# A decoder layer on one core: column means of two weights from a chunk sum, and v transposed at the head of a turn

## The chip, the core and the metric

The kernel runs on one core of one Trainium2 chip. The metric is the device time of one execution in microseconds (us). Engines are named as in the profile: PE is TensorE (PEld its weight loads), DVE is VectorE, ACT is ScalarE, POOL is GpSimd and SP is SyncE, which issues every DMA of this kernel. "L12" is line 12 of the kernel.

## The reference, cut to what matters

A decoder layer in float32 on x of shape (16, 256, 512): a state-space block, a long-convolution block over the other sequence, and a feed-forward block with eight low-rank experts, two of them chosen for each token. Each block is followed by a residual and a layer norm.

```python
x = layernorm(x + ssm(x, ...))
x = layernorm(x + conv_mix(x, k, fside_S2_0, ctx_2048, ctx_2048, 8))
x = layernorm(x + ffn(x, W, b, lora_A, lora_B, gate_w, gate_b))

def conv_mix(v, k, bias, x1, x2, num_heads):      # heads of 8 rows, 32 of them
    kv = vr[:, :, :, None, :] * x2r[:, :, None, :, :]
    y = causal_convolution(kv, k) + kv * skip
    out = einsum("bhijl,bhil->bhjl", y, x1r)

def ffn(x, W, b, lora_A, lora_B, gate_w, gate_b):
    base = x @ W.T + b
    logits = x @ gate_w.T + gate_b                # top 2 of 8, softmax over the two
    xA = einsum("nd,erd->ner", x, lora_A)
    out = base + sum over the chosen e of gate_e * (xA_e @ lora_B_e.T)
```

The layer norm ahead of the feed-forward block is not applied to its input. The kernel takes the column mean out of the weights instead, once: subtracting from each column of W.T (and of the gate and lora_A weights side by side) its mean over the 512 input rows has the same effect as subtracting each token's mean from x. The factor 1/std is multiplied in afterwards.

## The kernel before, in words

The order of the work is written out by hand: each engine executes its instructions in the order in which the code records them (`manual_schedule`), and waits only for data and for buffers. A buffer of a pool is given again when it is free; a new tile waits for the last reader of the tile before.

**First stage.** A loop over eight groups g of 512 tokens. In each group, ten steps i (the list `order`) form one pair of output blocks each, of the kinds x, z, b and c, by a seven-product scheme. Step i records `first_products` of its own pair (8 matmuls of 256 columns), then `finish_products` of the step before (6 matmuls), then the sums on DVE (`first_sums`, L357 to L361; `last_sums`, L371 to L373), and for the kind x the short convolution `mixed` (L571 to L580) into tiles `acc`, a tag of six buffers in pool p2. At step 6 `head_means(0)` (L585 to L596, matmul L589) reads four of these tiles, at step 8 `head_means(1)` the other four.

The weights of the feed-forward block, `w_f` (128 x 4 x 512: the 512 input rows as four chunks of 128 partitions) and `w_gl` (128 x 4 x 136, gates and lora_A), are loaded at the end of g = 0. In g = 1 they are prepared: at step 2 `with_identity` adds the residual's identity to w_f on DVE (L519, L521), and `centred` (L523 to L531) is called at the head of step 5 for w_f and of step 6 for w_gl. It forms the column means in one PSUM tile `mw` by four accumulating matmuls with `share`, a 128 x 128 matrix of 1/512, one for each chunk (L527), and subtracts the tile from each chunk on DVE (L531). POOL has only small operations in this part of g = 1.

**Second stage.** A loop over the 32 heads h (L1198), called turns below. In turn h, two halves q of the head's batch rows are convolved (`convolve`, L1005): matmuls with Toeplitz blocks of the taps, full 128 x 128 ones (L1014) and triangular ones as quadrants of 64 x 64 (L1032), into the PSUM tiles y[0] and y[1]. `contract` on DVE multiplies y by x1 (L1067) and sums (L1077). Meanwhile the feed-forward block of head h - 1 is done in pieces, and the products kv of head h + 1 are formed on DVE (L158) from vT and cT.

At the head of a turn with h > 0 the code records

- `feed_forward(base, o_r, (3,))`: the last of the four matmuls with w_f of head h - 2 (L1193), into PSUM tile `base`, where `rest` is not None (from h = 2);
- `turned_gates(xa)`: a transpose of the weighted low-rank activations on PE (L1183) and the copy `xaT` on ACT (L1185);
- `seeded(y, T, xs, 0)`: a matmul into `yc` (L1002), copied by ACT to both halves of y[1] (L1003), which the full matmuls of `convolve` add to;
- `lora(base, ...)`: a matmul that adds the low-rank part to base (L1189);
- `turned_v` for head h + 1: four transposes of the tile vn on PE (L146) and the copy vT on ACT (L148);
- the loads for later heads on SP: `load_T(h + 1)`, `load_v(h + 2)` into the single buffer of vn, `load_c(h + 2)`.

Then `convolve` for q = 0 begins with L1014 into y[0] and y[1]. The PSUM tiles of the transposes (vn, xa, the feed-forward input o_l at L1104) and of the gate logits `gl` share the two buffers of the tag "tr".

Of the kernel before, what the change touches and what calls it, by code (L numbers as in the profile page):

```python
# [8 lines left out]
F32 = mybir.dt.float32  # L9
AF = mybir.ActivationFunctionType  # L10
ALU = mybir.AluOpType
# [3 lines left out]
P = 128  # L15
B, S, D = 16, 256, 512
KD = D // P
# [14 lines left out]
NE, R = 8, 16  # L32
# [21 lines left out]
ER = NE * R  # L54
# [17 lines left out]
def decoder_kernel(  # L72
# [24 lines left out]
    nc = tc.nc  # L97
# [44 lines left out]
    def turned_v(vn):  # L142

        tr = ps_t.tile([P, NL, P], F32, tag="tr", name="tr")
        for k, blk in enumerate(BLOCKS_IN):
            nc.tensor.transpose(tr[:, k, :], vn[:, blk * P : (blk + 1) * P], ident)  # L146
        vT = q2.tile([P, NQ, NL, BQ * NH], F32, tag="vT", name="vT")
        nc.scalar.copy(  # L148
            vT.rearrange("p q k t -> p k q t"), tr.rearrange("p k (q t) -> p k q t", q=NQ)
        )  # L150
        return vT
# [29 lines left out]
    with ExitStack() as s1:  # L181
# [3 lines left out]
        p2 = s1.enter_context(tc.tile_pool(name="p2", bufs=2))  # L185
# [160 lines left out]
        def first_products(w, p, third, begun=None, between=None):  # L346

            al, be = begun or begin_products(w, p, third)
            product(be[:, 0:S], w, p, S1, "T1", start=True)
            if between is not None:  # L350
                between()
            product(al[:, S:], w, p, S2, "T2", stop=True)
            product(be[:, S:], w, p, S3, "T3", stop=True)
            return al, be
# [157 lines left out]
        def with_identity(w):  # L512

            for k, blk in enumerate(BLOCKS_OUT):
                own = w[:, k, blk * P : (blk + 1) * P]
                if blk in SWAPPED_OUT:
                    for a, b in ((0, HP), (HP, 0)):
                        half = own[:, a : a + HP]
                        nc.vector.tensor_tensor(half, half, ident[:, b : b + HP], ALU.add)  # L519
                else:  # L520
                    nc.vector.tensor_tensor(own, own, ident, ALU.add)  # L521

        def centred(w, cols):  # L523

            ps = ps_t.tile([P, 512], F32, tag="tr", name="mw")
            for kc in range(KD):
                nc.tensor.matmul(  # L527
                    ps[:, 0:cols], share, w[:, kc, :], start=(kc == 0), stop=(kc == KD - 1)
                )
            for kc in range(KD):  # L530
                nc.vector.tensor_tensor(w[:, kc, :], w[:, kc, :], ps[:, 0:cols], ALU.subtract)  # L531

# [6 lines left out]
                nc.sync.dma_start(first[sh][bi], r)  # L539

        heads = {}
        late = []
        for g in range(NG):
            xs = xs_next
            more = g + 1 < NG
# [39 lines left out]
            def head_means(ht):  # L585

                xm = ps_t.tile([P, GT], F32, tag="tr", name="xm")
                for q in range(4):
                    nc.tensor.matmul(  # L589
                        xm[32 * q : 32 * (q + 1), :],  # L590
                        mean.rearrange("p h n -> p (h n)"),
                        accs[4 * ht + q].rearrange("p b s -> p (b s)"),
                        start=True,
                        stop=True,
                    )
                return xm  # L596
# [44 lines left out]
            for i, (kind, p) in enumerate(order):  # L641
                if g == 1 and i == 2:
                    with_identity(w_f)
                if g == 1 and i in (5, 6):
                    centred(*((w_f, D), (w_gl, NE + ER))[i - 5])
                if i == 6:
                    ms = [head_means(0)]
                if g == 0 and i == 0:
                    al, be = first_products(
                        kinds[kind], p, True, None,  # L650
                        lambda: begun.append(begin_products(w_xi, order[1][1], False)),
                    )
                else:
                    al, be = first_products(
                        kinds[kind], p, i % 3 == 0, begun.pop(0) if begun else None
                    )
                if i == 8:
                    ms.append(head_means(1))
                if i == 9:


                    yps = ps_t.tile([P, S], F32, tag="tr", name="yps")
                    for ht in range(HT):
                        for b in range(GB):
                            nc.tensor.matmul(
                                yps[b * HP : (b + 1) * HP],
                                sel[:, ht].rearrange("p q h -> p (q h)"),
                                Bs[ht][:, b * S : (b + 1) * S],
                                start=(ht == 0),
                                stop=(ht == HT - 1),  # L670
                            )
                if before is not None:
                    finish_products()
                to = places(kind, p)
                u = first_sums(al, be, to)
                if i == 8:
                    states(1, stepped(ms[1], spreads[2]), spreads[3])
                if i == 6:
                    ms = [stepped(ms[0], spreads[0])]
                    spreads.append(spread(1, 1))  # L680
                if g == 0:
                    if i == 1:
                        parts = decays()
                    if i == 2:
                        nc.scalar.activation(A, A, AF.Exp)
                        nc.vector.tensor_scalar(A, A, -1.0, None, ALU.mult)
                    if i in (1, 2, 4):
                        next(parts)
                if i == 9:
                    yT = q3.tile([P, S], F32, tag="vn", name="yT", bufs=1)  # L690
                    nc.scalar.copy(yT, yps)
                if before is not None:
                    finish_sums((lambda: next(parts)) if g == 0 and i == 2 else None)
                if g == 0 and i == 3:
                    next(parts)
                if g == 0 and i in later:
                    for n, (w, k) in enumerate(later[i]):
                        ins = weight_sums(nc.gpsimd, w, k)
                        if n == 0:
                            wait_for(ins, mixes[-1])  # L700
                if i == 7:
                    states(0, ms[0], spreads[1])
                if i == 8:
                    outputs(0)
                    outputs(1)
                    if more:
                        rt = to_dram(rms(xs_next))
                    if g == 0:
                        behind = []
                        w_sums = w_o_sums(behind)  # L710
                        next(w_sums)
                before = (kind, p, al, be, u, to)
                if i < 2 and late:
                    normalised(g - 1, late.pop(0))
                if i == 1 and more:
                    xs_next = load_x(g + 1)
# [95 lines left out]
            late = []  # L812
            if more:
# [36 lines left out]
                late = [(1, xs[1]), (3, xs[3])]  # L850
            else:
                finish_sums()
                gated(1, spread_heads(1))
                for n, t in enumerate((0, 2, 1, 3)):


                    ps = ps_s.tile([P, 512], F32, tag="s", name="s") if n in (0, 3) else bank()
                    for c in range(NI):
                        for j in range(2):
# [4 lines left out]
                                start=(c == 0 and j == 0),  # L864
                                stop=(c == NI - 1),
# [14 lines left out]
            if g == 0:  # L880
                skip_bc = wp.tile([P, S], F32, name="skip_bc")
                nc.sync.dma_start(skip_bc, skip.partition_broadcast(P))
                w_gl = wp.tile([P, KD, NE + ER], F32, name="w_gl")
                nc.sync.dma_start(w_gl, WglT.rearrange("(k p) e -> p k e", p=P))
                w_f = wp.tile([P, KD, D], F32, name="w_f")
# [10 lines left out]
                share = wp.tile([P, P], F32, name="share")  # L896
# [5 lines left out]
    with ExitStack() as s2:  # L902
        w2 = s2.enter_context(tc.tile_pool(name="w2", bufs=1, reuse_waits="tile"))
        p2 = s2.enter_context(tc.tile_pool(name="r2", bufs=2, reuse_waits="tile"))
# [254 lines left out]
        vT_next, vns = heads["vT"], heads["vn"]  # L1159
# [38 lines left out]
        for h in range(HX):  # L1198
            nxt, ff = h + 1 < HX, last is not None
# [5 lines left out]
                prs = [multiplied(y_f, cT_f, 1, i) for i in order]  # L1205
            y = new_y()
            if h:
                if rest is not None:
                    base, o_r, xa = rest
                    feed_forward(base, o_r, (3,))  # L1210
                    turned = turned_gates(xa)
                seeded(y, T, xs, 0)
                if rest is not None:
                    lora(base, [turned])
                if nxt:
                    vT_after = turned_v(vns.pop(0))
                    kvs.append(load_T(h + 1))
                    if h + 2 < HX:
                        vns.append(load_v(h + 2))
                        cTs.append(load_c(h + 2))  # L1220
# [13 lines left out]
            if h == 0:  # L1234
                vT_after = vT_ahead[0]
# [212 lines left out]
```

## Time and profile before

| what | value |
|---|---|
| median of 3 runs | 1430.14 us (1429.83 to 1431.35) |
| span of the profiled execution | 1429.6 us; no further time of that execution is listed |
| PE busy, DVE busy | 1415.0 us (99%), 1215.5 us (85%) |
| ACT busy, POOL busy | 461.5 us (32%), 559.8 us (39%) |
| chain that ended last | PE for 96% of the span |
| granted TensorE clock | 0.999 |
| steps 2 to 6 of g = 1 | about 116 to 152 us from the span's start |
| second stage | from about 757 us |
| length of one turn | 20.61 us (L1183 from 1001.55 to 1022.16) |

The span is the time from the first to the last instruction in the profile, and the run times lie a little above it. A group of the profile names the line, the engine, the operation, and the tiles written and read. A float32 matmul leaves two MATMUL records, each with a weight load of its own; the records overlap, so that the time which a matmul holds TensorE is read from start to start. In a timeline, the columns are start, duration from the first to the last of the merged instructions, engine, line, operation, tiles, count, and in brackets the idle time before with what ended it. In a list of waits, the numbers are the total, the count and the longest.

### The profile page before, as it was taken

The numbers are of one execution on the slowest core, as the hardware profiler recorded it, in microseconds if no ns is written. First come the engines' busy times: TensorE is split into PE (matmuls) and PEld (weight loads), VectorE is DVE, ScalarE is ACT, GpSimd is POOL, SyncE is SP. The second block draws the span as 40 slices with busy tenths as digits, with TensorE's granted clock in tenths as the row PEclk, the third lists the DMA queues.
The fourth block names the chain that finished last, engine by engine and source line by source line (L and its number), as shares of the span: only waits on it lengthen the run. The fifth ranks groups of instructions, "written<-read, shape, count | busy, mean of one in ns | idle before, by whom it ended". The sixth has DMA issues, their size and how long they took to land.

```text
span 1429.6 us, 19152 instructions
## 1 busy us (share of the span) xinstructions
PE 1415.0 (99%) x6956; PEld 913.5 (64%) x6956; DVE 1215.5 (85%) x2102; ACT 461.5 (32%) x964; POOL 559.8 (39%) x655
## 2 busy tenths in 40 slices
PE   8999999999999999999999999999999999999997
PEld 7888788787888888888884444444444444444443
DVE  6988778877888787877848999999999999999996
ACT  2423323233232332322312333333333333333331
POOL 5450010100100201001004776677677767766772
PEclk9999999999999999999999999999999999999999
DMA  8014021120121201212003212221221222122200
GB/s 300 33 38 131 16 75 46 38 83 8 56 68 42 74 17 39 83 45 88 15 18 114 71 53 81 74 67 64 82 74 61 69 74 81 60 70 74 80 30 23
DMA packets 49167, 93.38 MB, mean 65 GB/s; under 512 B 8880, under 2 KB 13360, under 8 KB 49072
## 3 DMA queue, kind: packets, MB, share of 16 engines
q1 hardware_dynamic: 49072, 92.15, 20.0%
q8 instruction: 55, 0.90, 0.3%
q14 instruction: 40, 0.33, 0.1%
HBM read 74.82 MB, written 17.32 MB: 64 GB/s over the span
## 4 chain that ended last, share of the span: by engine, by line
PE 96%; DVE 1%; issue 1%; POOL 1%; DMA 0%; SPq 0%; POOLq 0%; ACT 0%; DVEq 0%; ACTq 0%
PE mm L329 20%; PE y L1014 15%; PE s L329 14%; PE y L1032 12%; PE base L1193 8%; PE s L769 6%; PE mm L769 6%; PE yc L1002 4%; PE gl L1270 2%; PE base L1189 2%; PE tr L1104 1%; PE mm L726 1%; PE xm L589 1%; PE mm L860 1%; PE tr L146 1%
## 5 line engine op out<-in xcount | busy, mean ns | idle before, releaser
L1067 DVE TENSOR_TENSOR pr<-y,cT 128x1024 f32<-128x1024 f32 x126 | 148.4, 1219 | 40.4 <-PE y L1032 37.2
L158 DVE TENSOR_TENSOR kv<-vT,cT 128x1024 f32<-128x1024 f32 x128 | 179.4, 1442 | 1.5 <-ACT vT L148 1.5
L1032 PE MATMUL y<-kv 64*64 64x512 f32 x1408 | 179.7, 598 | 0.0
L578 DVE SCALAR_TENSOR_TENSOR acc<-xi,wc,acc 128x512 f32<-128x512 f32 x192 | 142.3, 754 | 7.4 <-ACT acc L574 1.7
L1077 DVE TENSOR_REDUCE red<-pr 128x128 f32<-128x1024 f32 x126 | 147.1, 1208 | 0.0
L1014 PE MATMUL y<-kv 128*128 128x512 f32 x272 | 127.9, 593 | 1.0 <-ACT y L1003 1.0
L1032 PEld LDWEIGHTS y<-kv 64*64 64x64 f32 x1408 | 51.2, 132 | 119.4 <-issue 91.0
L950 POOL TENSOR_TENSOR o<-t,vT 64x384 f32<-64x384 f32 x64 | 121.9, 1905 | 4.4
L1193 PE MATMUL base<-w_f,ol 128*128 128x512 f32 x248 | 119.5, 605 | 0.0
L1014 PE MATMUL y<-kv,Td 128*128 128x512 f32 x248 | 116.5, 592 | 0.0
L67 POOL TENSOR_TENSOR rs_a<-ve_a,nhalf 128x1 f32<-128x1 f32 x32 | 19.0, 594 | 243.1 <-DVE ve_a L65 243.1
L390 POOL TENSOR_TENSOR rstd<-ms,nhalf 128x4 f32<-128x4 f32 (+1 forms) x9 | 8.5, 947 | 260.6 <-DVE ms L388 260.6
L329 PE MATMUL mm<-XT,w_z 128*128 128x256 f32 x384 | 90.7, 379 | 0.0
L1014 PEld LDWEIGHTS y<-kv,Td 128*128 128x128 f32 x248 | 47.1, 190 | 59.3 <-issue 59.3
L979 POOL TENSOR_TENSOR xs<-kv 128x512 f32<-128x512 f32 x63 | 81.3, 1290 | 2.4
L1014 PEld LDWEIGHTS y<-kv 128*128 128x128 f32 x272 | 48.9, 190 | 51.9 <-issue 48.7
L329 PEld LDWEIGHTS mm<-XT,w_z 128*128 128x128 f32 x384 | 73.0, 190 | 9.9
L1193 PEld LDWEIGHTS base<-w_f,ol 128*128 128x128 f32 x248 | 42.3, 189 | 54.5 <-issue 54.5
L1003 ACT COPY y<-yc 128x1024 f32<-128x1024 f32 x62 | 61.8, 997 | 32.9 <-PE yc L1002 23.9
L329 PE MATMUL mm<-xnT,w_z 128*128 128x256 f32 x288 | 71.0, 382 | 0.0
L1225 POOL TENSOR_TENSOR ol<-o,red 128x512 f32<-128x512 f32 x31 | 39.4, 1271 | 79.3 <-DVE red L1077 79.1
L1032 PE MATMUL y<-kvd,kv 64*64 64x512 f32 x128 | 65.2, 589 | 0.0
(278 smaller groups left out, 2940.3 us busy)
## 6 DMA issues: line engine op xcount, KB each, us to landing
cT<-in_ctxT SPq DMA_DIRECT2D x32, 448.0 KB
kv<-in_toep SPq DMA_DIRECT2D x32, 448.0 KB
xt<-in_x SPq DMA_DIRECT2D x32, 256.0 KB
spread<-both SPq DMA_DIRECT2D x32, 256.0 KB
first<-xt SPq DMA_DIRECT2D x32, 256.0 KB
vn<-first SPq DMA_DIRECT2D x32, 256.0 KB
out<-res SPq DMA_DIRECT2D x31, 256.0 KB
xnT<-in_xT SPq DMA_DIRECT2D x7, 1024.0 KB
```

What stands on the lines that cost most here:

```text
L158: last = nc.vector.tensor_tensor(kv[:, q, k * BQ : (k + NL // 2) * BQ], vT[:, q, blks].rearrange("p k (b i) -> p (k b) i", i=NH).unsqueeze ...
L329: nc.tensor.matmul(ps, w[:, p, a, kc, :], Xs[b][:, kc, :], start=start and kc == 0, stop=stop and kc == 1, skip_group_check=upon,)
L578: ins = nc.vector.scalar_tensor_tensor(acc, xi[:, :, k : k + S], wc[:, c, k : k + 1], acc, ALU.mult, ALU.add)
L769: nc.tensor.matmul(ps, own[a][c][:, n * P : (n + 1) * P], w_o[b][c], start=start and c == 0, stop=stop and c == HC - 1, skip_group_check=upon,
L950: nc.gpsimd.tensor_tensor(o[b : b + HP, :, 0:3], t[a : a + HP, :, 1:4], vT[a : a + HP, :, 1:4], ALU.add,)
L979: return nc.gpsimd.tensor_tensor(xs[:, q], moving(kv, q, 0), moving(kv, q, 1), ALU.add)
L1003: nc.scalar.copy(y[1], yc.unsqueeze(1).to_broadcast([P, 2, BQ * NH * NH]))
L1014: nc.tensor.matmul(bank_of(y, lb), w, moving(kv, q, mb), start=not late and lb not in begun, stop=False, skip_group_check=True,)
L1032: return nc.tensor.matmul(bank_of(y, lb)[cols], T[rows, at, cols], src[rows], start=start, stop=False, skip_group_check=True,)
L1067: nc.vector.tensor_tensor(pr.rearrange("p (k b j) i -> p k b j i", k=2, j=NH), y[i].rearrange("p k (b j i) -> p k b j i", j=NH, i=NH), cT[ ...
L1077: nc.vector.tensor_reduce(red[:, q, 2 * i : 2 * i + 2, :].rearrange("p k t -> p (k t)"), pr, AX.X, ALU.add)
L1193: nc.tensor.matmul(base, o_l[:, kc, :], w_f[:, kc, :], start=(first and kc == kcs[0]), stop=False)
```

## The change

`centred` no longer multiplies each chunk. A new function `chunk_sum` adds the four chunks of a weight on POOL (three additions) into a tile `w_sum` of the tag "acc", and `centred` forms the means from that sum by one matmul. The sums are recorded at the heads of steps 3 (w_f) and 4 (w_gl) of g = 1; `centred` follows one step after each, at steps 4 and 5 instead of 5 and 6. In the second stage, `turned_v` is recorded ahead of `feed_forward(base, o_r, (3,))` instead of behind `lora`; the loads keep their place in the code.

```diff
-        def centred(w, cols):
+        def chunk_sum(w, cols):
+
+            total = p2.tile([P, D], F32, tag="acc", name="w_sum", bufs=6)[:, 0:cols]
+            nc.gpsimd.tensor_tensor(total, w[:, 0, :], w[:, 1, :], ALU.add)
+            for kc in range(2, KD):
+                nc.gpsimd.tensor_tensor(total, total, w[:, kc, :], ALU.add)
+            return total
+
+        def centred(w, cols, total):
 
             ps = ps_t.tile([P, 512], F32, tag="tr", name="mw")
-            for kc in range(KD):
-                nc.tensor.matmul(
-                    ps[:, 0:cols], share, w[:, kc, :], start=(kc == 0), stop=(kc == KD - 1)
-                )
+            nc.tensor.matmul(ps[:, 0:cols], share, total, start=True, stop=True)
             for kc in range(KD):
                 nc.vector.tensor_tensor(w[:, kc, :], w[:, kc, :], ps[:, 0:cols], ALU.subtract)
...
-        late = []
+        late, sums = [], []
...
-                if g == 1 and i in (5, 6):
-                    centred(*((w_f, D), (w_gl, NE + ER))[i - 5])
+                if g == 1 and i in (3, 4):
+                    w, cols = ((w_f, D), (w_gl, NE + ER))[i - 3]
+                    total = chunk_sum(w, cols)
+                if g == 1 and i in (4, 5):
+                    centred(*sums.pop(0))
+                if g == 1 and i in (3, 4):
+                    sums.append((w, cols, total))
...
             if h:
+                if nxt:
+                    vT_after = turned_v(vns.pop(0))
                 if rest is not None:
                     base, o_r, xa = rest
                     feed_forward(base, o_r, (3,))
...
                 if rest is not None:
                     lora(base, [turned])
                 if nxt:
-                    vT_after = turned_v(vns.pop(0))
                     kvs.append(load_T(h + 1))
```

## The prediction, made before the changed kernel ran

> **What bounds the kernel now.** I read the page from the top: the busy shares, then the chain that ended last, then TensorE's own waits, then the timelines of the two places that the diff touches.
>
> ```profile
> PE 1415.0 (99%) x6956; PEld 913.5 (64%) x6956; DVE 1215.5 (85%) x2102; ACT 461.5 (32%) x964; POOL 559.8 (39%) x655
> PE 96%; DVE 1%; issue 1%; POOL 1%; DMA 0%; SPq 0%; POOLq 0%; ACT 0%; DVEq 0%; ACTq 0%
> PE yc L1002 <- POOL xs L979: 1.4, 1, 1.4
> PE y L1014 <- ACT y L1003: 1.0, 1, 1.0
> ```
>
> TensorE is busy for 1415.0 of 1429.6 us, and the chain is TensorE for 96%. In the waits of PE nothing exceeds 1.8 us; between 130 and 744 us there is no entry at all, and the two above lie at the start of the second stage. So matmul time that is removed comes off the end, and a new wait of TensorE is added to it, as long as the other engines keep up. (DVE, at 85%, is the one to watch.)
>
> The first place is g = 1, TensorE's timeline. A float32 matmul leaves two records.
>
> ```profile
> 128.15 1.03 PE L329 MATMUL mm<-xnT,w_z 128*128 128x256 f32 x4
> 129.01 2.75 PE L329 MATMUL mm<-XT,w_z 128*128 128x256 f32 x12
> 131.60 1.89 PE L329 MATMUL s<-xnT,w_xi 128*128 128x256 f32 x8
> 133.33 1.03 PE L329 MATMUL s<-XT,w_xi 128*128 128x256 f32 x4
> 134.19 3.60 PE L527 MATMUL mw<-w_f,share 128*128 128x512 f32 x8
> 137.62 1.03 PE L329 MATMUL mm<-xnT,w_xi 128*128 128x256 f32 x4
> ...
> 143.67 1.09 PE L527 MATMUL mw<-w_gl,share 128*128 128x136 f32 x8
> 144.69 1.07 PE L589 MATMUL xm<-acc,mean 128*32 128x512 f32 x8
> ```
>
> Read starts, not durations: the four matmuls of w_f hold TensorE from 134.19 to 137.62, 3.43 us; those of w_gl from 143.67 to 144.69, 1.02 us, of which I count 0.93 (0.09 goes with the switch to the 32-column matmul L589).
>
> The second place is the head of each head-loop turn, with the middle of a turn below it for comparison.
>
> ```profile
> 999.62 1.04 PE L1032 MATMUL y<-kv 64*64 64x512 f32 x8
> 1000.59 1.12 PE L1193 MATMUL base<-w_f,ol 128*128 128x512 f32 x2
> 1001.55 0.27 PE L1183 MATMUL xat<-ident,xa 128*128 128x128 f32 x1
> 1001.66 1.02 PE L1002 MATMUL yc<-xs,kv 128*128 128x512 f32 x2
> 1002.52 1.02 PE L1189 MATMUL base<-w_lb,xaT 128*128 128x512 f32 x2
> 1003.38 0.60 PE L146 MATMUL tr<-ident,vn 128*128 128x128 f32 x4
> 1003.82 1.88 PE L1014 MATMUL y<-kv 128*128 128x512 f32 x4
> ...
> 1009.12 1.04 PE L1032 MATMUL y<-kv 64*64 64x512 f32 x8
> 1010.08 0.66 PE L1104 MATMUL tr<-ident,ol 128*128 128x128 f32 x4
> 1010.58 1.02 PE L1002 MATMUL yc<-xs,kv 128*128 128x512 f32 x2
> ```
>
> A 512-column matmul takes 0.86 from start to start (1002.52 to 1003.38). The base one behind the 64x64 quadrants takes 0.96 (1000.59 to 1001.55). Four transposes take 0.44 (1003.38 to 1003.82), but 0.50 behind the quadrants (1010.08 to 1010.58). So **whatever stands first behind the quadrants pays: about 0.10 if it is a base matmul, 0.055 if it is a transpose**. In the line's durations this is 592/592/697 ns for L1193, and 328 against 273 ns for the transpose.
>
> **What the Trainium skill says.** "TensorEngine Tiling (Array Packing)", Key Properties: changing the tiling mode drains TensorE. The trace agrees: L1032's last two rounds take 0.97 to the base matmul, and about 0.43 a round elsewhere. "TensorE: Matmul & The Clock Gate", Step-by-step: weight loads are pulled ahead of running matmuls. Here the load for xat starts at 1001.13, 0.42 ahead of its matmul, but the load of the first base matmul starts with it, at 1000.59. A base load lasts 190 ns, a transpose's 140: the part that is not hidden differs by the 50 ns found above. "GPSIMD Engine Reference", Specifications: GpSimd shares its SBUF interfaces with VectorE, and contends with VectorE instructions of two SBUF inputs or a two-port mode. The trace agrees: the same 128x512 op on POOL lasts 1272 to 1560 ns (L222).
>
> **Part 1, the column means.** Removed: three of four matmuls twice. w_f: 3/4 of 3.43 = 2.57 us; w_gl: 3/4 of 0.93 = 0.70; together **-3.27**. Added on POOL: three 128x512 adds and three 128x136. By L222 to L228 one lasts 1.27 to 1.33, and one that waits for its forerunner starts 0.08 after it. The small ones lie between L948 (128x128, 0.46) and L232 (128x256, 0.73). POOL has nothing else between 123.4 and 167.6, so 6 us fit, if they are in time.
>
> For w_f they are just not. The adds wait for with_identity on DVE, whose lines are
>
> ```profile
> 123.92 0.62 DVE L519 TENSOR_TENSOR w_f<-w_f,ident 128x64 f32<-128x64 f32 x4
> 124.47 0.48 DVE L521 TENSOR_TENSOR w_f<-w_f,ident 128x128 f32<-128x128 f32 x2
> ```
>
> POOL starts at 124.6, after the fourth L519; three adds of 1.28 with two gaps of 0.08 end at 128.6. The matmul now stands ahead of step i = 4, which TensorE reaches at 128.15. **New wait:** 128.65 - 128.15 = 0.50, plus 0.1 for a weight load that nothing hides, so +0.6. Behind it on TensorE waits everything. Bounds: 0 if the adds take 1.1 (L935's 1.08 is the fastest 128x512 on POOL); 1.3 if each takes 1.5. I take 0.6, since beside them DVE has mostly PSUM operands (L359 to L373). The sum for w_gl ends near 130.5 and is used near 136: nothing.
>
> DVE's subtractions are as many as before, but 2.4 (w_f) and 0.9 (w_gl) come one step earlier, while TensorE runs 2.7 ahead. The tightest places: the sums of step 4 (L359 to L361) move from 134.85 to 137.25 and end at 138.6, needed by TensorE at 139.4 and 140.3; those of step 5 end at 145.5 and 146.5, needed at 146.6 and 147.4. About 1 us is left, from 4 to 5 us before. After that DVE idles for TensorE as it did (1.89 at 148.98, 1.05 at 152.03), so the lead is kept. The two sums take two of the six acc buffers; the built order has ACT's L579 for the sixth convolution tile wait for the w_gl matmul, near 136, but its input is only ready near 139: nothing. Part 1: -3.27 + 0.6 = **-2.7** (-3.3 to -2.0).
>
> **Part 2, v turned first.** Moved: four transposes on TensorE, the copy L148 (0.59) on ACT to ahead of xaT (L1185) and y (L1003), and with it the point at which SP may issue load_v and load_c; load_T, ahead of them in SP's queue, stays. TensorE's work is the same, in order tr, base, xat, yc, lora, y. The transposes now pay 0.055 behind the quadrants and base no longer pays 0.105: **-0.05 a turn**. That is for h = 2 to 30, 29 turns: -1.45. At h = 1 TensorE waits for POOL's xs anyway and then for ACT's y: 0.
>
> What must not break is ACT's copy into y[1], which the second L1014 matmul waits for.
>
> ```profile
> 1001.86 0.27 ACT L1185 COPY xaT<-xat 128x128 f32<-128x128 f32 x1 [1.50 <-PE xat L1183]
> 1002.77 1.00 ACT L1003 COPY y<-yc 128x1024 f32<-128x1024 f32 x1 [0.64 <-PE yc L1002]
> 1004.07 0.59 ACT L148 COPY vT<-tr 128x512 f32<-128x512 f32 x1 [0.31 <-PE tr L146]
> ```
>
> It ends at 1003.77; the matmul starts at 1003.82 + 0.86 = 1004.68, a cover of 0.9. All between base and lora moves 0.4 later, so the copy ends at 1004.2: cover 0.5, less 0.2 for the weight load. L148 runs at 1001.4 to 1002.0, in ACT's idle 1.50, and xat comes at 1002.0, so L148 delays nobody. xaT is late by as much as lora. xa, done at 1000.8, gains cover. The x3 sum on DVE (L1144, 1005.28) needs lora by then: done near 1004. vn lands with most of a 20.6 us turn to spare. DVE idles 1.26 a turn for TensorE, so a turn 0.05 shorter is not taken by DVE. Part 2: **-1.45** (+1 to -1.6).
>
> **Sum:** -2.7 - 1.45 = -4.1 on the span of 1429.6. No time of the profiled execution is listed apart; the median, 1430.14, lies 0.5 above the span, and I take the same from it: **1426.0 us**. No change that can be told is within 0.2%, 2.9 us: 1427.3 to 1433.0.
>
> **Rivals.**
> 1. Part 2 moves nothing: the transposes behind the quadrants pay 0.1 too, with the extra wait for vn's transfer there. L1104's 0.50 speaks against it, but L1104 waits for POOL, not for a transfer. Then -2.7: 1427.4.
> 2. POOL is later than I think (1.5 us an add, later starts), or DVE's 1 us of slack is used up and TensorE stops at step 5 or 6. Part 1 loses 2 us or more: 1428.0 to 1428.7.
> 3. Slower: the y[1] copy becomes the wait of each turn. Decides when it ends over 0.3 later than worked out, at 1004.5. Each 0.1 beyond costs 29 x 0.1 = 2.9 us. With 0.5 us beyond, +14.5 less 2.7 and less 1.45: 1440.5. For it: the cover falls from 0.9 to 0.5, and ACT works in order, so a late L148 (it also waits for POOL's L950) would hold xaT and y. Against it: L950 ends at 1018.77, some 2.9 us ahead of where L148 now comes.
> 4. The change does not do what it says: the order of the built kernel shows one matmul each, and the transposes first, so only its timing is open.
>
> **Numbers.** As forecast 0.63 (1425.0 to 1427.2, the bounds of the POOL wait and of part 2's saving with some 0.3 of scatter), rival 1 0.14, rival 2 0.12, rival 3 0.08, a larger gain 0.03. Rival 1 lies on the 0.2% edge and I split it. Faster 0.74, same 0.18, slower 0.08. Leaving out rival 3 and the edges, the range is 1424.9 to 1428.8.
>
> **What would show it.** L527's successor with 2 records for each weight; the first started near 128.7 instead of 128.15, with a wait of about 0.6 on POOL; L589 of g = 1 at 142.0. In a turn, L1193's maximum duration at 592 to 600, L146's at 328, a turn of 20.56 instead of 20.61 us, and ACT's y at +0.4 behind the turn's start with no wait of L1014 for it. A wait of L1014 for ACT in every turn, or of L329 for DVE near 139 to 147, would prove me wrong.

## The result, and the profile after

The changed kernel takes **1494.8 us** in the median against 1430.14 us before: a ratio of 1.0447, interval 1.0434 to 1.0461. I had forecast 1426.0. One of its five runs took 2110.24 us at a granted clock of 0.655; the others lie between 1493.67 and 1495.24, and the ratio uses these alone. The profiled span went from 1429.6 to 1493.5 us, 63.9 more. Part 1 (the column means) and TensorE's side of part 2 (v turned first) came as worked out; a third thing, which I had not looked for, costs 2.34 us in 29 of 30 turns.

The page of the kernel after: the busy shares, the chain that ended last by engine, and three groups (busy us, mean ns | idle before). L1077 of after is L1067 of before.

```profile
PE 1432.4 (96%) x6944; PEld 908.4 (61%) x6944; DVE 1285.4 (86%) x2102; ACT 461.1 (31%) x964; POOL 559.7 (37%) x661
PE 69%; DVE 11%; POOL 5%; issue 3%; ACT 3%; DMA 0%; POOLq 0%; ACTq 0%; SPq 0%; DVEq 0%
L158 DVE TENSOR_TENSOR kv<-vT,cT 128x1024 f32<-128x1024 f32 x128 | 202.3, 1619 | 1.4 <-ACT vT L148 1.4
L1077 DVE TENSOR_TENSOR pr<-y,cT 128x1024 f32<-128x1024 f32 x126 | 148.2, 1217 | 38.4 <-issue 38.4
L960 POOL TENSOR_TENSOR o<-t,vT 64x384 f32<-64x384 f32 x64 | 91.7, 1433 | 4.4
```

The same three groups of the kernel before:

```profile
L1067 DVE TENSOR_TENSOR pr<-y,cT 128x1024 f32<-128x1024 f32 x126 | 148.4, 1219 | 40.4 <-PE y L1032 37.2
L158 DVE TENSOR_TENSOR kv<-vT,cT 128x1024 f32<-128x1024 f32 x128 | 179.4, 1442 | 1.5 <-ACT vT L148 1.5
L950 POOL TENSOR_TENSOR o<-t,vT 64x384 f32<-64x384 f32 x64 | 121.9, 1905 | 4.4
```

The operations and their counts are the same, so DVE has no more work, yet it is busy for 70 us more. Its product kv, which nobody edited, is 177 ns longer in the mean, while POOL's add of the same stretch is 472 ns *shorter*. DVE's other product of the same size, pr, has one input in PSUM and did not change. The chain is now TensorE's for 69% of the span, in place of 96%; it leaves for DVE, POOL and ACT in the long turns, one of which is shown below.

TensorE's waits after (total us, times, longest):

```profile
PE xat L1193 <- DVE xa L1141: 39.3, 30, 1.7
PE y L1024 <- DVE pr L1077: 5.4, 30, 0.2
PE y L1024 <- ACT y L1013: 1.0, 1, 1.0
PE mw L534 <- POOL w_sum L528: 0.5, 1, 0.5
```

The first two lines are new in the turns, 30 times each (before, xat waited once, for 0.9). The third is the old single wait: the copy into y[1], my rival 3, does not appear in the turns. The fourth is the wait for POOL that I had put at 0.6.

**Part 1** in TensorE's timeline of after:

```profile
128.72 1.13 PE L534 MATMUL mw<-w_sum,share 128*128 128x512 f32 x2 [0.52 <-POOL w_sum L528]
...
135.72 0.40 PE L534 MATMUL mw<-w_sum,share 128*128 128x136 f32 x2
...
142.09 1.07 PE L594 MATMUL xm<-acc,mean 128*32 128x512 f32 x8
```

The xm matmul starts at 142.09 instead of 144.69: 2.60 earlier. That is the forecast, 142.0, and so is the start at 128.72 (forecast 128.7).

**A turn.** TensorE's timeline of after, at the head of one turn:

```profile
1018.53 0.66 PE L146 MATMUL tr<-ident,vn 128*128 128x128 f32 x4
1019.02 1.02 PE L1203 MATMUL base<-w_f,ol 128*128 128x512 f32 x2
1021.35 0.30 PE L1193 MATMUL xat<-ident,xa 128*128 128x128 f32 x1 [1.30 <-DVE xa L1141]
1021.49 1.08 PE L1012 MATMUL yc<-xs,kv 128*128 128x512 f32 x2
1022.41 1.02 PE L1199 MATMUL base<-w_lb,xaT 128*128 128x512 f32 x2
1023.62 1.95 PE L1024 MATMUL y<-kv 128*128 128x512 f32 x4 [0.18 <-DVE pr L1077]
```

The transposes stand first, and the base matmuls L1203 last 593 ns in the mean of the page instead of 605, as forecast. Then TensorE stands still, because xa is late. So what made xa late? DVE's timeline over the preceding stretch, before:

```profile
1014.77 3.15 DVE L158 TENSOR_TENSOR kv<-vT,cT 128x1024 f32<-128x1024 f32 x2
...
1018.17 0.69 DVE L1120 TENSOR_TENSOR cmp<-lg 128x64 f32<-128x64 f32 x1
1018.78 0.21 DVE L1121 TENSOR_TENSOR cmp<-lg 128x64 f32<-128x64 f32 x1
1018.92 1.28 DVE L1122 TENSOR_TENSOR cmp<-cmp,tri 128x64 f32<-128x64 f32 x1
...
1020.63 0.20 DVE L1126 SCALAR_TENSOR_TENSOR ex<-rank,ex 128x8 f32<-128x8 f32 x1
...
1021.08 0.35 DVE L1131 SCALAR_TENSOR_TENSOR xa<-gl,den,ex 128x128 f32<-128x128 f32 x1
```

and after:

```profile
1012.16 3.94 DVE L158 TENSOR_TENSOR kv<-vT,cT 128x1024 f32<-128x1024 f32 x2
...
1016.35 0.96 DVE L1130 TENSOR_TENSOR cmp<-lg 128x64 f32<-128x64 f32 x1
1017.24 0.77 DVE L1131 TENSOR_TENSOR cmp<-lg 128x64 f32<-128x64 f32 x1
1017.92 1.53 DVE L1132 TENSOR_TENSOR cmp<-cmp,tri 128x64 f32<-128x64 f32 x1
...
1019.88 0.73 DVE L1136 SCALAR_TENSOR_TENSOR ex<-rank,ex 128x8 f32<-128x8 f32 x1
...
1020.86 0.35 DVE L1141 SCALAR_TENSOR_TENSOR xa<-gl,den,ex 128x128 f32<-128x128 f32 x1
```

From the start of the products to the end of xa it is 1021.43 - 1014.77 = 6.66 us before and 1021.21 - 1012.16 = 9.05 after. POOL beside it, before:

```profile
1014.81 3.96 POOL L950 TENSOR_TENSOR o<-t,vT 64x384 f32<-64x384 f32 x2
1018.85 1.27 POOL L979 TENSOR_TENSOR xs<-kv 128x512 f32<-128x512 f32 x1
```

and after:

```profile
1012.10 2.92 POOL L960 TENSOR_TENSOR o<-t,vT 64x384 f32<-64x384 f32 x2
1015.10 2.13 POOL L989 TENSOR_TENSOR xs<-kv 128x512 f32<-128x512 f32 x1
1017.19 0.72 POOL L994 TENSOR_TENSOR Td<-kv 128x256 f32<-128x256 f32 x1
1017.88 1.49 POOL L928 TENSOR_TENSOR sk<-kv,skip_bc 128x512 f32<-128x512 f32 x1
1019.33 1.26 POOL L989 TENSOR_TENSOR xs<-kv 128x512 f32<-128x512 f32 x1
```

Three readings.

1. **Who is first has changed.** Before, DVE's products start 0.04 us ahead of POOL's adds (1014.77, 1014.81). After, POOL starts 0.06 ahead (1012.10, 1012.16). The lines merge two operations each; in the trace's single records the first product takes 1.22 and POOL's first add 2.03 when DVE leads; 2.01 and 0.99 when POOL leads.
2. **The small gate operations end when POOL ends.** These are the operations that choose the two experts of each token (L1120 to L1131 before, L1130 to L1141 after). After, the four of them with two SBUF inputs end at 1017.31, 1018.01, 1019.45 and 1020.61, and POOL's four operations behind the adds end at 1017.23, 1017.91, 1019.37 and 1020.59. Each DVE operation ends 0.02 to 0.10 behind one of POOL. Before, two of the four meet one (1018.86 behind POOL's 1018.77, and 1020.20 behind 1020.12). POOL has come through its adds earlier, so its next operations now lie across the gate's. This is read from the times of the ends; no run tests the gate's part apart from the products'.
3. **Together** the two account for the whole: 0.79 in the products (3.94 - 3.15) and 0.27 + 0.56 + 0.25 + 0.53 = 1.61 in the gate make 2.40, and 9.05 - 6.66 is 2.39.

The Trainium skill says this exactly, on a page that I had not drawn on: "SBUF — State Buffer", Who interferes with whom. A DVE instruction with two SBUF inputs contends with a GpSimd instruction that reads SBUF; the one that issues first has the pair of SBUF ports that the two engines share for the whole instruction, and the other blocks. "Issue order, not op shape, decides who blocks." The traces agree, with a small difference: the product starts 0.06 into POOL's add of 0.99, so it should be blocked for the 0.93 that are left and then take its own 1.22, together 2.15 (an estimate from these durations); it takes 2.01.

What it costs a turn: xa ends 11.35 behind the transposes L1104 before (1021.43 - 1010.08), and 13.80 behind L1114 after (1021.21 - 1007.41), 2.45 later. TensorE would want it for the xat matmul at 12.47 (the base matmuls' start at 11.61, and 0.86) and starts that at 13.94: a stop of 1.47. The rest of the turn is in the chain that ended last (start, us, what; after, same turn):

```profile
1020.86 0.35 DVE xa L1141
1021.21 2.26 DVE pr L1077 x2
...
1025.87 1.27 POOL ol L1236
1027.13 1.19 POOL nm_c L1100
...
1029.15 0.09 ACT one L1058
1029.25 0.04 issue
1029.29 1.09 PE y L1042 x8
```

Behind xa everything on DVE is late: pr stops L1024 by 0.35 (0.775 from the start of the last L1199 matmul record to the first of L1024, in place of 0.43), and the way over POOL and ACT stops L1042 by 0.31. Against the same turn of e3, an experiment below that keeps TensorE's order without the stops, the matmuls behind the three stops take 0.09, 0.08 and 0.05 longer. In all 1.47 + 0.35 + 0.31 + 0.22 = 2.35; turns last 22.90 instead of the 20.56 that TensorE alone would need. 29 such turns are 29 x 2.34 = 67.9, less the 4.1 that I had forecast as gain, 63.8, against 63.9 between the two spans and 64.7 between the medians.

### The profile page after: what moved, and what is told of

It is laid out like the page before. It is cut to its first block, busy times and chain, and to the rows that moved or that the text cites. A ratio compares the mean times of both kernels' runs of the same rounds, so it can differ in the third digit from the quotient of the medians.

```text
span 1493.5 us, 19165 instructions
## 1 busy us (share of the span) xinstructions
PE 1432.4 (96%) x6944; PEld 908.4 (61%) x6944; DVE 1285.4 (86%) x2102; ACT 461.1 (31%) x964; POOL 559.7 (37%) x661
## 4 chain that ended last, share of the span: by engine, by line
PE 69%; DVE 11%; POOL 5%; issue 3%; ACT 3%; DMA 0%; POOLq 0%; ACTq 0%; SPq 0%; DVEq 0%
PE mm L329 16%; PE s L329 11%; PE y L1042 8%; PE y L1024 8%; PE base L1203 5%; PE s L779 5%; PE mm L779 5%; DVE pr L1077 5%; DVE red L1087 3%; POOL ol L1236 2%; POOL nm_c L1100 2%; PE gl L1281 2%; PE yc L1012 2%; ACT sq L1105 1%; DVE ex L1136 1%
## 5 line engine op out<-in xcount | busy, mean ns | idle before, releaser
L158 DVE TENSOR_TENSOR kv<-vT,cT 128x1024 f32<-128x1024 f32 x128 | 202.3, 1619 | 1.4 <-ACT vT L148 1.4
L1042 PE MATMUL y<-kv 64*64 64x512 f32 x1408 | 185.8, 602 | 3.5
L1077 DVE TENSOR_TENSOR pr<-y,cT 128x1024 f32<-128x1024 f32 x126 | 148.2, 1217 | 38.4 <-issue 38.4
L1024 PE MATMUL y<-kv 128*128 128x512 f32 x272 | 130.2, 601 | 6.4 <-DVE pr L1077 5.4
L1042 PEld LDWEIGHTS y<-kv 64*64 64x64 f32 x1408 | 48.6, 132 | 131.8 <-issue 90.9
L1203 PE MATMUL base<-w_f,ol 128*128 128x512 f32 x248 | 116.6, 593 | 0.0
L1024 PE MATMUL y<-kv,Td 128*128 128x512 f32 x248 | 116.5, 592 | 0.0
L989 POOL TENSOR_TENSOR xs<-kv 128x512 f32<-128x512 f32 x63 | 105.8, 1680 | 2.4
L1024 PEld LDWEIGHTS y<-kv 128*128 128x128 f32 x272 | 48.8, 189 | 81.3 <-issue 48.9
L960 POOL TENSOR_TENSOR o<-t,vT 64x384 f32<-64x384 f32 x64 | 91.7, 1433 | 4.4
L1024 PEld LDWEIGHTS y<-kv,Td 128*128 128x128 f32 x248 | 47.1, 190 | 59.3 <-issue 59.3
L1105 ACT ACTIVATE sq<-x,nm_c 128x512 f32<-128x512 f32 x31 | 22.4, 721 | 142.5 <-POOL nm_c L1100 142.5
L1012 PE MATMUL yc<-xs,kv 128*128 128x512 f32 x124 | 65.4, 609 | 0.8 <-POOL xs L989 0.8
```

Source lines behind the costliest of these rows:

```text
L158: last = nc.vector.tensor_tensor(kv[:, q, k * BQ : (k + NL // 2) * BQ], vT[:, q, blks].rearrange("p k (b i) -> p (k b) i", i=NH).unsqueeze ...
L960: nc.gpsimd.tensor_tensor(o[b : b + HP, :, 0:3], t[a : a + HP, :, 1:4], vT[a : a + HP, :, 1:4], ALU.add,)
L989: return nc.gpsimd.tensor_tensor(xs[:, q], moving(kv, q, 0), moving(kv, q, 1), ALU.add)
L1012: nc.tensor.matmul(yc, T[:, 2, :], xs[:, q], start=True, stop=True)
L1024: nc.tensor.matmul(bank_of(y, lb), w, moving(kv, q, mb), start=not late and lb not in begun, stop=False, skip_group_check=True,)
L1042: return nc.tensor.matmul(bank_of(y, lb)[cols], T[rows, at, cols], src[rows], start=start, stop=False, skip_group_check=True,)
```

## The experiments

My theory after reading this, called A in the expectations: the race of DVE's product and POOL's add sets the turn, and part 2 turned it. Rivals were B, that part 1 shifts the second stage, and C, that TensorE's new order itself is too late for something. The table has what each run gave (medians over the 30 turns of its trace, us; starts are counted from the turn's transposes, L1104 or its counterpart; the lead is POOL's start ahead of DVE's). Each run was compared with runs of the kernel before on its own chip, medians 1430.04 to 1430.41.

| kernel | DVE product starts | POOL add starts | POOL's lead | product, add last | turn | median us, ratio [95%] |
|---|---|---|---|---|---|---|
| before | 4.687 | 4.729 | -0.04 | 1.22, 2.03 | 20.61 | 1430.14 |
| after | 4.744 | 4.682 | 0.06 | 2.01, 0.99 | 22.90 | 1494.8, 1.0447 [1.0434, 1.0461] |
| e1_sums_alone | 4.688 | 4.725 | -0.04 | 1.22, 2.03 | 20.61 | 1427.69, 0.9983 [0.9977, 0.9990] |
| e2_turn_alone | 4.743 | 4.681 | 0.06 | 2.01, 0.99 | 22.90 | 1499.5, 1.0484 [1.0468, 1.0500] |
| e3_copy_behind | 4.687 | 4.725 | -0.04 | 1.22, 2.03 | 20.56 | 1426.07, 0.9970 [0.9959, 0.9982] |
| e4_pool_pause | 4.744 | 4.831 | -0.09 | 1.22, 1.98 | 20.57 | 1426.48, 0.9974 [0.9963, 0.9984] |
| e5_dve_pause | 4.827 | 4.725 | 0.10 | 1.16, 2.11 | 20.61 | 1430.36, 1.0001 [0.9992, 1.0009] |
| e6_before_pool_pause | 4.687 | 4.872 | -0.19 | 1.22, 1.88 | 20.61 | 1430.23, 1.0001 [0.9992, 1.0009] |
| e7_copy_behind_pause | 4.687 | 4.874 | -0.19 | 1.21, 1.88 | 20.57 | 1426.39, 0.9973 [0.9963, 0.9983] |
| e8_short_pause | 4.743 | 4.715 | 0.027 | both kinds | 20.57 or 22.93 | 1455.29, 1.0170 [1.0148, 1.0193] |
| e9_dve_reduce | 4.779 | 4.724 | 0.06 | 2.02, 0.99 | 22.93 | 1507.62, 1.0541 [1.0525, 1.0556] |
| e10_both_pauses | 4.779 | 4.869 | -0.09 | 1.22, 1.98 | 20.61 | 1430.23, 1.0000 [0.9991, 1.0009] |

**The two parts alone.** e1_sums_alone is the diff without its last two hunks (part 1), e2_turn_alone is those two hunks on the kernel before.

> Only the column means are changed; v is turned where it was before. Theory A (the loss is an order race in the turns: VectorE's second pair of kv products and GpSimd's add of the residual start within 0.05 us of each other, and who starts first keeps the shared SBUF interface; moving the transposes changed who is first): untouched turns of 20.61 us, products at +4.69 us and GpSimd's add at +4.73 us behind L1104's transposes, and the shift of 2.6 us from the first stage, so 1427.5 us. Theory B (the shift of the second stage by the first part, or the changed buffers of the first stage, brought the slow turns): slow turns of 22.9 us here too, near 1496 us.

> Only the place of the transposes of v is changed; the column means are formed as before. Theory A: slow turns of 22.9 us, GpSimd's add at +4.68 us and the products at +4.74 us behind L1104's transposes, so the time of the changed kernel plus the 2.6 us that the column means save: 1497.4 us. Theory B: turns of 20.56 us, 1428.7 us.

Part 1 alone gains 2.5 us and leaves the turns as they were. Part 2 alone has all of the loss. B is out. The 2 us by which e2 misses its 1497.4 are about one turn: all 30 are long here, and 29 in the kernel after.

**The copy put back.** e3_copy_behind keeps part 1, and the transposes first on TensorE, but ACT's copy vT is recorded behind `lora`, where it was:

```diff
     def turned_v(vn):
...
+        return tr
+
+    def copied_v(tr):
         vT = q2.tile([P, NQ, NL, BQ * NH], F32, tag="vT", name="vT")
...
-                    vT_after = turned_v(vns.pop(0))
+                    tr_after = turned_v(vns.pop(0))
...
                     lora(base, [turned])
                 if nxt:
+                    vT_after = copied_v(tr_after)
```

> The changed kernel with one thing undone: TensorE transposes v at the head of the turn, but ScalarE's copy of it into vT is recorded behind lora again, hence behind the copies of xaT and y. Theory A in full (the extra semaphore wait of VectorE's multiplication for ScalarE's y copy, needed only because the vT copy no longer stands behind the y copy on ScalarE, is what makes VectorE the second): the products start at +4.69 us and GpSimd's add at +4.73 us as before, turns of 20.56 us, 1426.1 us. Theory C (the order on TensorE itself is what hurts: base, lora and xa's transpose 0.44 us later make the x3 sum, ScalarE's one or xa late): slow turns stay, 1490 us or more.

Its page, in the busy shares and the two groups (its lines stand 3 further down):

```profile
PE 1410.1 (99%) x6944; PEld 913.2 (64%) x6944; DVE 1215.5 (85%) x2102; ACT 458.8 (32%) x964; POOL 564.9 (40%) x661
...
L161 DVE TENSOR_TENSOR kv<-vT,cT 128x1024 f32<-128x1024 f32 x128 | 179.3, 1440 | 1.4 <-ACT vT L151 1.4
L963 POOL TENSOR_TENSOR o<-t,vT 64x384 f32<-64x384 f32 x64 | 122.0, 1907 | 4.4
```

1426.07, faster than both kernels: the whole forecast gain of 4.1 us, with turns of 20.56. TensorE's new order is harmless, which puts C out; the place of one ACT copy decides. Why? In the built programs, each engine waits only for what an earlier wait has not already told it. Before, DVE's product for q = 0 waits for the vT copy, which stands behind the y copy on ACT, so that this wait covers the y copy too, and pr (L1067) waits for two semaphores. After, the vT copy is ahead of the y copy; pr (L1077) needs a third wait, on ACT, and starts 0.219 behind the transposes instead of 0.163. In the traces, too, the record of pr names a semaphore of PE before and of ACT after. The y copy had long been done (in the turn of the prediction it ended at 1003.77, and pr starts at 1010.25): what costs 56 ns is having the wait, not waiting. The last turn, which has no next head and so no vT copy, shows it in the kernel before too: pr at 0.219. DVE's queue carries the 56 ns to the second products (4.687 to 4.744). On ACT the opposite happens: the y copy of q = 1 has one wait fewer, and POOL, released by ACT's sq behind it (L1105), starts var_b at 3.33 instead of 3.38, and the add 0.047 earlier. The lead moves by 0.056 + 0.047 = 0.10, from -0.04 to +0.06.

**POOL held back by work.** e4_pool_pause is the kernel after with one useless operation on POOL in each `with_residual`, and e6_before_pool_pause the same on the kernel before (`pause` is a float32 tile of 128 x 128):

```diff
         def with_residual(t, vT):
+            nc.gpsimd.memset(pause, 0.0)
```

> The changed kernel with one more instruction a turn: a memset of 128x128 on GpSimd, read by nobody, ahead of the add of the residual, which makes that add about 0.2 us later. Theory A: VectorE's products start first again, by 0.14 us; TensorE no longer waits for xa, turns of 20.56 us, 1426.1 us although work was added. Theory C, or a loss that comes from VectorE's or ScalarE's longer waits as such: no gain, 1494 us or some 6 us more.

> The kernel before, with the memset of 128x128 on GpSimd ahead of its add of the residual, the control to the changed kernel with it. Theory A: VectorE is first already, so nothing is gained: turns of 20.61 us, 1430.1 us. If the pause were good for another reason (fewer collisions later in the turn), it would gain here too.

Added work takes 68 us off the kernel after, with the diff otherwise complete: DVE's product is first again, and the turn is at TensorE's 20.57. On the kernel before, where DVE is first anyway, the same work changes nothing. This shows the cause most directly: the 56 ns on DVE are still there (4.744), only the order is back. With it the wait for xa is gone from the turns (one of 0.9 in the whole of e4's trace), and the gate's operations have their old lengths. e7_copy_behind_pause, the memset on top of e3, asks whether a larger lead of DVE brings more.

> Both remedies at once: v's copy recorded behind lora and the memset on GpSimd. Theory A: VectorE leads by some 0.19 us instead of 0.04, and the turn stays at 20.56 us, 1426.1 us; the lead only has to be there, more of it gives nothing. If the loss grew steadily with the distance of the two, this one would be faster than either remedy alone.

It does not: 1426.39 and turns of 20.57. Between leads of 0.04 and 0.19 the margin makes no difference; the order is what matters.

**DVE held back, a miss.** e5_dve_pause puts a memset of the same size on DVE in the kernel before, ahead of the second products:

```diff
             if nxt:
+                nc.vector.memset(pause, 0.0)
                 products(vT_next, cT_n, kv_n, 1)
```

> The kernel before, with one more instruction a turn: a memset of 128x128 on VectorE, read by nobody, between the reductions and the second pair of kv products. It delays these products by about 0.1 us or more, and their lead over GpSimd's add is only 0.04 us. Theory A: GpSimd starts first, the first product lasts 2.0 instead of 1.2 us, turns of some 22.9 us, near 1497 us, without any change of TensorE's order. Theory C (the order of TensorE's work is what hurts): VectorE has over 1 us of idle time a turn, so 1430 us, or 1433 at most.

I expected the long turns, and got 1430.36 with turns of 20.61. DVE's product starts 0.10 behind POOL's add and is short all the same, while the add takes 2.11. Either my theory was wrong, or DVE had the pair already through the memset (A1 in the expectations), against A2, that DVE keeps its place as long as it has any instruction waiting or running. e9_dve_reduce tells them apart by an operation with one SBUF input and a result of 128 x 1; e10_both_pauses adds the POOL memset of e6 to it.

```diff
             if nxt:
+                nc.vector.tensor_reduce(spare, ident[:, 0:32], AX.X, ALU.add)
                 products(vT_next, cT_n, kv_n, 1)
```

> The kernel before, with a small reduction (128x32 to 128x1, one SBUF operand, its result read by nobody) on VectorE between its reductions and the second pair of kv products. In the run with the memset there, VectorE kept its place although its product was recorded later than GpSimd's add. Theory A1 (the memset itself held the shared interface until the product; what decides is whether an instruction of VectorE that uses it is running or 0.03 us away when GpSimd's add arrives): a one-operand reduction, like L1077, does not hold it, so GpSimd's add goes first, the product lasts 2.0 us, turns near 22.9 us, some 1495 us. Theory A2 (VectorE keeps its place for as long as it has any instruction waiting or running): turns of 20.61 us, 1430.2 us.

> The same small reduction on VectorE, and the 128x128 memset on GpSimd ahead of its add, which puts that add 0.14 us later. The control to the run with the reduction alone: if that one is slow, this one has the same work on VectorE but GpSimd second again. Theory A1: turns of 20.61 us, 1430.2 us. If the reduction itself costs the time, this one is as slow as the other.

The same groups on the page of e9, where POOL leads by 0.06:

```profile
L158 DVE TENSOR_TENSOR kv<-vT,cT 128x1024 f32<-128x1024 f32 x128 | 203.5, 1629 | 1.5 <-ACT vT L148 1.5
L950 POOL TENSOR_TENSOR o<-t,vT 64x384 f32<-64x384 f32 x64 | 90.9, 1420 | 4.4
```

and on that of e10, where DVE leads by 0.09:

```profile
L158 DVE TENSOR_TENSOR kv<-vT,cT 128x1024 f32<-128x1024 f32 x128 | 179.4, 1442 | 1.5 <-ACT vT L148 1.5
L951 POOL TENSOR_TENSOR o<-t,vT 64x384 f32<-64x384 f32 x64 | 120.6, 1884 | 4.4
```

The kernel before, with nothing of the diff in it, loses 78 us through one DVE operation of 0.175 us a turn, and has them all back when POOL gets a delay too. A2 is out. This speaks for A1, and so does the memset's own start in e5, 4.746, only 0.02 behind POOL's add, a distance at which DVE still comes first in e8 below. That the memset held the pair is still an inference, not seen by itself: a product that reads its inputs ahead of its recorded start, when what runs before it reads nothing, would look the same, and no run here separates the two. The size was missed in e9: 1495 expected, 1507.6 measured. The expectation was some 5 us too low by its own reasoning: 30 turns longer by 2.33 on 1430.0 are 1499.9. Of the 29 turns ahead of the last, 24 last 22.87 to 22.96, as worked out; four last 24.3 and one 23.2, another 5.7 us. That gives 1505.6, against 1505.9 for the run in the profile; the other three took 1507.5 to 1508.0, at clocks of 0.992 and 0.993 (0.995 in the profile, 0.999 before). Why the five turns are longer stays open.

**The border.** e8_short_pause is e4 with a pause of 128 x 1, which delays POOL by only 0.03.

> The changed kernel with a shorter pause, a memset of 128x1 on GpSimd. The one-column memsets of the kernel before follow each other every 0.044 us, so GpSimd's add would come at about +4.73 us, still ahead of the products at +4.74. Theory A: who is first decides, not by how much: slow turns of 22.9 us, near 1494 us, while the 128x128 pause gave 1426. If it lands behind +4.74 us, fast turns of 20.57 us, 1426.3 us. A gradual loss would give something between.

Neither an all-long nor an all-short kernel came out: the trace has 10 long turns (22.86 to 22.95) and 20 short ones (20.56 to 20.57, and the last, which is 20.17 in the kernel before too), and none between. By the records, POOL's lead is 0.024 to 0.028 in the short ones (and -0.23 in one), 0.028 to 0.035 in the long ones. So the outcome is either-or, with the border at a lead of about 0.028, and a few nanoseconds decide on 2.36 us. If being first decides, a border that isn't at 0 says that a recorded start is not exactly the moment that counts. 10 x 2.36 = 23.6 on top of e4's span of 1424.5 gives 1448.1, the span of this profile. It would also explain why this kernel's runs scatter from 1449.9 to 1457.5, by some three long turns; only the fastest of them was traced. By this border neither shift alone would have turned the race (DVE's 56 ns alone: a lead of 0.014; POOL's 47 ns alone: 0.005). That is worked out and wasn't tried.

## Why the prediction was wrong

- **Part 1: right.** -3.27 + 0.6; measured -2.60 at the xm matmul, a wait of 0.52 for POOL, and e1's 2.5 us. DVE's last 1 us of lead held; rival 2 did not come.
- **Part 2 on TensorE: right.** The saving behind the quadrants is the forecast 0.05 (20.56 against 20.61 in e3), and e3 gives 4.1 for both parts, the sum as worked out. Rival 1 is refuted.
- **The y[1] copy: right.** L1024 has no wait for ACT in the turns. Rival 3, my only way to a slower kernel, was the wrong one.
- **The step that failed** is in part 2: "L148 delays nobody", which put the cost of the moved copy at nothing. It holds for data: nobody waits longer for L148. "DVE idles 1.26 a turn" is true as well, and no help: the idle time (1.18 after) lies ahead of pr, not between the products and xa. But I asked of a moved instruction only when it runs, not which other waits its place had made unnecessary. Its move gave DVE a wait, took one from ACT, and shifted two engines by 0.056 and 0.047 against each other. That put POOL's add ahead of DVE's product, and cost 2.34 us in each of 29 turns.
- **Why so little mattered:** I had cited the sharing of the interfaces, and used it for part 1's adds alone. The turn had the warning in it: in the kernel before, L950's first add takes 2.03 beside DVE's products and 0.99 in the last turn, which has none, and the two start 0.04 apart. A race with so thin a margin needed a rival of its own. The first part of its price was in reach, the product lengthened by POOL's add of about 1 us; the larger part, in the gate, would have needed POOL's later operations laid beside DVE's.
- "xa, done at 1000.8, gains cover" took xa's time as fixed. Its cover was 1.0 (wanted at 12.47, done at 11.35, some 0.14 from the end of xa to the matmul), against 2.45 of delay.

What remains open: why in turn 6 of the kernel after POOL's adds come 0.26 late. The delay begins at ACT's y copy, which starts at 1.81 behind the transposes instead of 1.55, and the adds of the same turn are late by about as much in e1, e4 and e8. In the kernel after, DVE is first in this turn alone: its product is short, and the turn lasts 20.57, an experiment that came for free.

## What to carry to other kernels

When an instruction moves in one engine's order, compare the built waits of every engine before and after: a wait that an earlier one had covered can come back elsewhere, and here it cost 56 ns though what it waited for was long done. Then look for places where DVE operations with two SBUF inputs and POOL operations start close together, and write down who is first and by how much; here a lead of 0.04 us was turned over by moving one copy. If the order matters, make it safe. e3 keeps both parts of the change and restores the order by where the copy is recorded, but DVE leads by the same thin 0.04 as before; e7 adds work on POOL and widens the lead to 0.19 at no cost that can be told (1426.07 and 1426.39; e4, with 1426.48, can't be told from them either).

## What the runs showed of the hardware that I had not expected

- A POOL lead of 24 to 28 ns by the records still leaves DVE first, one of 28 to 35 ns does not (e8). The second one loses most of the winner's duration: 0.79 us on the product beside an add of 0.99, 1.04 on the add beside a product of 1.22.
- The two orders are not symmetric in what follows. After the products, POOL's early finish puts its next four operations over DVE's gate, and there DVE operations that take as little as 0.17 to 0.22 elsewhere in these traces take 0.73 to 1.53 (before, 0.20 to 1.29).
- A third semaphore wait, long fulfilled, delayed a DVE instruction by 56 ns (0.163 to 0.219).
- A useless memset of 0.20 us a turn on POOL made a kernel 68 us faster (e4).
